# Layer 0's front with TensorE in a written order: pairs of tiles mixed on quarter blocks, and a tail written out by hand on all engines

## The chip, the cores and the metric

The kernel runs on one core of a Trainium2 chip. The core has a matrix engine (TensorE, PE), a vector engine (VectorE, DVE), a scalar engine (ScalarE, ACT), a general engine (GpSimd, POOL) and an engine that issues transfers (SyncE, SP); every engine works through its own queue of instructions in order and waits on semaphores for the others. Matmuls read from the on-chip memory SBUF and write to PSUM, which has eight banks of 512 f32 columns on 128 partitions.

The metric is the time of the whole program on the device, in microseconds. The kernel before took 2567.02 us in the median of three runs (2560.18 to 2570.76).

## The reference

The program computes four layers, each a conditional linear map ("cond") followed by a block ("ffn"), on 2048 tokens of 512 numbers, all in f32. The change lies in layer 0 and, by one constant, in the front of layer 1. Layer 0 is this:

```python
# cond: sequences of 64 tokens, each with its own 64x64 weights, over the tokens
w = weights[conditions]                       # 200 sets of weights, 32 sequences
x = einsum('bct,bcd->bdt', x, w)              # B, 64, 512
# attention, sequences of 64 here (causal), 16 heads of 32
n = rmsnorm(x, ln1)
kv, q = n @ kv_d_w, n @ q_d_w                 # latents of 128
k = concat(kv @ k_u_w, rope(n @ rope_k_w));  q = concat(q @ q_u_w, rope(q @ rope_q_w))
h = x + (softmax(mask(q k^T / sqrt(32))) @ (kv @ v_u_w)) @ o_w
# mixture of experts: one shared expert, two of seven routed ones per token
n = rmsnorm(h, ln2)
probs = sigmoid(n @ router_w + router_b);  scores, idx = top_k(probs, 2)
out = h + shared(n) + sum_k scores_k / sum(scores) * expert[idx_k](n)
# expert(x) = (silu(x @ wg) * (x @ wu) / 8) @ wd, inner size 256
```

Layer 1 begins with a cond of the same form (8 sets of weights), and a router with 32 experts, four per token.

## The kernel before, in words

The 2048 tokens are 16 tiles (NT) of 128 tokens, that is, two sequences a tile. Layer 0 has a *front* (class `Front`), which does all up to the routing of every tile, then an expert stage, which gathers the rows that belong to each expert (`xr`, L361, issued on POOL), multiplies them (gu L1191, y L1204) and writes them out.

The front is a software pipeline. A loop over 19 steps calls 13 methods in each step, each for the tile of its own lag (table `turns`): lag 0 is the newest tile, lag 3 the oldest. In the order of the table: `mix` (0), `values` (2), `qk_turn` (1), `norm_turn` (0), `out_turn` (2), `gate_up` (3), `scores` (1), `latents` (0), `out` (2), `down` (3), `qkv` (0), `probs_turn` (1), `out_norm` (2). Apart from that the tile framework's planner sets the order of each engine's queue; it moves instructions by what it takes their costs to be.

What the methods are, with the line that the profile shows:

- `mix` (L605): both 64x64 weights of a tile are gathered into `wsel` (L361, POOL), and POOL lays them out as a 128x128 matrix with two blocks on its diagonal (`wbd`, L418, two operations). One matmul of 128x128 weights with 512 columns, in two f32 passes, mixes the tile. ScalarE copies it to `h` (L607); `rms_scaled` squares it on ScalarE (L395), VectorE scales the sum (ms, L397), POOL takes the power (rstd, L385) and VectorE makes `xn` (L400).
- `turn` (L587) transposes a tile by four matmuls into one bank; VectorE (L589, L593) or ScalarE (L591) copies it to SBUF. `norm_turn` turns xn, `qk_turn` q and k (qT, kT), `probs_turn` the probabilities (sT), `out_turn` the attention's result, `out_norm` the normed `hn`.
- `latents` is lp (L631, 16 passes), `qkv` is qp (L644 to L650) and vp (L669: four matmuls with 128x64 weights, two column halves), `scores` is sp (L698) and the softmax on VectorE (L703, m L708, the subtraction L709, den L712) and ScalarE (exp L710). `values` is ap (L731), 64x64 weights in the four quarters of the array; VectorE divides (att, L738, two halves). `out` is op (L756), eight passes of 512 columns, then the sum, the norm and the store of `hn` as a row of `rows`.
- `gate_up` is the router's matmul rp (L776, tile name tok), sigmoid (L781), the two largest (`choose`, L969 and L970), and the shared expert's gate and up (gu, L506). `down` is the shared expert's y (L796), and after every second tile the `put`.
- `put` (L976 to L1004, L941 to L964) counts where each token of two tiles goes: VectorE makes `hot` (L979), `sel` (L984), `pre` (L986); two matmuls (L989, L990) count; VectorE goes on with the count to the one-hot tables `a` and `b` (L950), ScalarE scales `a` (L961), and four f16 matmuls (`total`, L963) add to the lists of tokens, which `end` casts to `stok`. The gathers of the expert stage read `stok`.

The tag "one" in PSUM has three banks for mix, tp, lp, vp, op, gu and y together; "big" has two pairs of banks for qp, sp and ap; one bank holds the router's and the put's small results.

Tiles in LATER (6 to 13) leave out the shared expert in the front: it is done afterwards, for the first two (GAP) in the gap before layer 1, for the others in *pieces* between the steps of layer 1's front (class `Mixed`, L243 in the profile, `fill`): six pieces a tile, four of gu and two of y. Tiles in SPLIT (0 to 10) have their router's matmul in layer 1 done as four column parts of 32 (`parts`), copied by ScalarE and added by a second matmul; the others have one direct matmul.

`g.held` is a set of engines whose instructions stay in the order in which the program gives them; `g.nc` leaves the order to the planner.

Of the kernel before, what the change touches and what calls it, by code (L numbers as in the profile page):

```python
# [21 lines left out]
P = 128  # L22
# [21 lines left out]
LATER = range(6, NT - 2)  # L44
LEAD = 6
GROUPS = {3: 4, 7: 4, 11: 4, 13: 2, 15: 2}
SPLIT = range(11)
# [98 lines left out]
def _layout(i):  # L146
# [7 lines left out]
    a["cond0"] = i["itok_B_1_198"].reshape(NT, 2).T  # L154
# [269 lines left out]
def layer0(g, w3, pool3):  # L424
    tc, nc, a = g.tc, g.nc, g.a
    with ExitStack() as ctx:
# [6 lines left out]
        with ExitStack() as c1:  # L433
# [3 lines left out]
            x = [g.load_x(sb, a["x"], i, 5) for i in range(3)]  # L437
# [8 lines left out]
            f = Front(g, sb, ps, w, br, ln2, at0, m, x, xs, shared)  # L446

            turns = (
                ("mix", 0), ("values", 2), ("qk_turn", 1), ("norm_turn", 0), ("out_turn", 2), ("gate_up", 3),
                ("scores", 1), ("latents", 0), ("out", 2), ("down", 3), ("qkv", 0), ("probs_turn", 1),  # L450
                ("out_norm", 2),
            )
            for step in range(NT + 3):
                if step >= 4:
                    clear()
                if step in (15, 17):
                    m.weights((step - 15) // 2)
                for stage, lag in turns:
                    if 0 <= step - lag < NT:
                        getattr(f, stage)(step - lag)  # L460
            m.end(sb)
        m.ready(ctx)
# [103 lines left out]
class Front:  # L566
# [3 lines left out]
    def __init__(self, g, sb, ps, w, br, ln2, at, m, x, xs, shared):  # L570
        self.shared = shared
        self.g, self.sb, self.ps, self.w, self.br, self.ln2 = g, sb, ps, w, br, ln2
        self.at, self.m, self.x, self.xs = at, m, x, xs
        self.held = {}
# [7 lines left out]
    def turn(self, src, dst, act, scale=None):  # L582
# [3 lines left out]
        for c in range(4):  # L586
            nc.tensor.transpose(tp[:, c, :], src[:, c * P : (c + 1) * P], self.g.ident)  # L587
# [7 lines left out]
    def mix(self, i):  # L595
        g, nc, sb = self.g, self.g.nc, self.sb
        if i == 0:
            self.weights(0)
            self.lay()
        wbd = self.wbd  # L600
        if i >= len(self.x):
            self.x.append(g.load_x(sb, g.a["x"], i, 5))
        x = self.x[i]
        o = self.ps.tile([P, D], F32, name="mix", tag="one")
        nc.tensor.matmul(o, wbd, x, start=True, stop=True)  # L605
        h = sb.tile([P, D], F32, name="h", bufs=4)
        nc.scalar.copy(h, o)  # L607
        self.keep(i, x=x, h=h, xn=g.rms_scaled(sb, h, "xn", True))
        self.weights(i + 1)

    def weights(self, i):

        self.asked = self.g.cond_weights(self.sb, "wc0", self.at, i) if i < NT else None

    def lay(self):
        if self.asked:
            self.wbd = self.asked(self.sb.tile([P, P], F32, name="wbd"))
# [7 lines left out]
    def latents(self, i):  # L625
# [3 lines left out]
        for j in range(2):  # L629
            for c in range(4):  # L630
                nc.tensor.matmul(  # L631
                    lp[:, j, :], w["w_lat"][:, c, j * P : (j + 1) * P], xnT[:, c, :], start=c == 0, stop=c == 3
                )
# [3 lines left out]
        self.lay()  # L637

    def qkv(self, i):
        g, nc, sb, w = self.g, self.g.nc, self.sb, self.w  # L640
# [3 lines left out]
        nc.tensor.matmul(qp[:, 0, :], lat[:, 1, :], w["w_q"], start=True, stop=True)  # L644
        kv = qp[:, 1, :].rearrange("p (h z d) -> p z h d", h=16, z=2)
        nc.tensor.matmul(
            kv[:, 0], lat[:, 0, :], w["w_kn"].rearrange("p (h d) -> p h d", h=16), start=True, stop=True
        )
        for c in range(4):
            nc.tensor.matmul(  # L650
# [16 lines left out]
        for b in range(2):  # L667
            for odd in range(2):
                nc.tensor.matmul(  # L669
# [15 lines left out]
    def scores(self, i):  # L685
# [5 lines left out]
        for rr in range(2):  # L691
            sp = self.ps.tile([P, 2, D], F32, name="sp", tag="big", bufs=2)
            for r2 in range(2):
                q0 = 32 * (2 * rr + r2)
                for c in range(4):
                    for b in range(2):
                        cols = slice(64 * b, 64 * b + 64)
                        nc.tensor.matmul(  # L698
# [12 lines left out]
        den = sb.tile([P, 16], F32, name="den", bufs=3)  # L711
        nc.vector.tensor_reduce(den, s, AX.X, ALU.add)  # L712
        nc.vector.reciprocal(den, den)
        self.keep(i, s=s, den=den)
# [8 lines left out]
    def values(self, i):  # L723
# [3 lines left out]
        for j in range(8):  # L727
            for odd in range(2):
                rows = slice(64 * odd, 64 * odd + 64)
                for b in range(2):  # L730
                    nc.tensor.matmul(  # L731
# [18 lines left out]
    def out(self, i):  # L750

        g, nc, sb = self.g, self.g.nc, self.sb
        attT, h, x = self.take(i, "attT", "h", "x")
        op = self.ps.tile([P, D], F32, name="op", tag="one")
        for c in range(4):
            nc.tensor.matmul(op, attT[:, c, :], self.w["w_o"][:, c, :], start=c == 0, stop=c == 3)  # L756
        nc.vector.tensor_tensor(h, h, op, ALU.add)
        hn = g.rms_scaled(sb, h, "hn")
# [12 lines left out]
    def gate_up(self, i):  # L771
        g, nc, sb, w = self.g, self.g.nc, self.sb, self.w
        (hT,) = self.take(i, "hnT")
        rp = self.m.bank[:, 448 : 448 + E0]
        for c in range(4):
            nc.tensor.matmul(rp, hT[:, c, :], w["w_r0"][:, c, :], start=c == 0, stop=c == 3)  # L776
        lg = sb.tile([P, E0], F32, name="lg")
        nc.vector.tensor_tensor(lg, rp, self.br, ALU.add)
        probs = sb.tile([P, 8], F32, name="probs")
# [3 lines left out]
        if i == NT - 1:  # L783
            self.m.put(self.sb, i - 1, 2)
        if i not in LATER:
            self.shared.hT[i] = hT
            self.shared.up(sb, self.ps, i, "one")

    def down(self, i):
        nc = self.g.nc  # L790
        if i not in LATER:
            (x,) = self.take(i, "x")
            act = self.shared.acts.pop(i)
            y = self.ps.tile([P, D], F32, name="y", tag="one")
            for ic in range(2):
                nc.tensor.matmul(y, act[:, ic, :], self.w["w_shd"][:, ic, :], start=ic == 0, stop=ic == 1)  # L796
            nc.vector.tensor_tensor(x, x, y, ALU.add)
            nc.sync.dma_start(out=self.xs[i * P : (i + 1) * P, :], in_=x)
        if i % 2 and i < NT - 1:
            self.m.put(self.sb, i - 1, 2)  # L800
# [44 lines left out]
class Moe:  # L845
# [90 lines left out]
    def mark(self, sb, ps, tok, sl, slot, ov, i, n, tiles):  # L936
# [1830 lines left out]
```

## Time and profile before

| what | value |
|---|---|
| median of three runs | 2567.02 us (2560.18 to 2570.76) |
| profiled execution | 2568.85 us |
| its span, and what lies around it | 2567.1 us and 1.75 us |
| mean granted TensorE clock | 0.975 |
| TensorE busy | 2430.8 us (95% of the span) |
| VectorE, ScalarE, GpSimd busy | 1408.3, 715.5, 908.4 us |
| steady part of layer 0's front, 60 to 345 us | TensorE busy 274.69 of 285 us |
| end of the front and first experts, 345 to 396 us | TensorE busy 39.23 of 51 us, clock 0.74 |
| layer 1's front, 640 to 700 us | TensorE 50.14, VectorE 50.10 of 60 us |
| start of the values of tile 14 (ap, the first work of the last steps) | 331.94 us |
| first gather of rows for the experts | 376.21 us |

How to read it: PE is the matmul, PEld the load of its weights, which runs beside the matmuls. Every f32 matmul is two records, since it is two passes. A line of a timeline has the start in us, the busy time, engine, line, operation, result and inputs, the shapes, and in square brackets the idle time of the engine just before with what ended it. A line of the waits has in the end the sum in us, how often, and the longest. In the rows by stretches each engine has its busy us and, in parentheses, its number of instructions; behind them stand the granted clock (1 is full speed), the share of the DMA engines and GB/s.

### The profile page before, as it was taken

How to read it: one execution, taken by the hardware profiler on the slowest of the kernel's cores; microseconds unless marked ns; L12 is line 12 of the kernel's file. 1: busy time of each engine (PE TensorE's matmuls, PEld its weight loads, DVE VectorE, ACT ScalarE, POOL GpSimd, SP SyncE). 2: the span in 40 equal slices, each digit the busy share in tenths (PEclk: the TensorE clock that was granted, in tenths of full speed). 3: DMA queues.
4: the chain of work that ended last, by engine and by line, in shares of the span. 5: the costliest groups of instructions: out<-in, count | busy, mean ns of one | idle time of the engine just before them, and what ended most of it. 6: DMA issues, size and time to landing. Idle time of an engine off the chain costs nothing.

```text
span 2567.1 us, 42539 instructions
## 1 busy us (share of the span) xinstructions
PE 2430.8 (95%) x16597; PEld 1624.3 (63%) x16597; DVE 1408.3 (55%) x3470; ACT 715.5 (28%) x1480; POOL 908.4 (35%) x961
## 2 busy tenths in 40 slices
PE   6999989998889999969999999999999999979998
PEld 4776766665566666746666666666666665435665
DVE  4667656832855554436554444455444432557887
ACT  2444420111311111101322222222222221236664
POOL 2223225613243444533333333333333212573440
PEclk9999989999989999989999999999999999989999
DMA  2334325435556877844222222222222213523551
GB/s 102 105 126 169 112 71 196 157 133 175 202 170 230 344 275 255 293 161 163 66 77 76 76 76 73 73 73 73 76 77 76 82 55 135 166 69 110 146 143 54
DMA packets 132570, 339.40 MB, mean 132 GB/s; under 512 B 23993, under 2 KB 25049, under 8 KB 125056
## 3 DMA queue, kind: packets, MB, share of 16 engines
q1 hardware_dynamic: 90720, 188.84, 21.5%
q0 software_dynamic: 41056, 141.89, 17.5%
q10 hardware_dynamic: 576, 5.77, 0.6%
q8 instruction: 136, 2.23, 0.4%
q14 instruction: 82, 0.67, 0.1%
HBM read 245.23 MB, written 107.22 MB: 137 GB/s over the span
## 4 chain that ended last, share of the span: by engine, by line
PE 50%; DVE 2%; POOL 1%; issue 1%; DMA 1%; ACT 0%; SPq 0%; ACTq 0%; POOLq 0%; DVEq 0%
PE out L2138 9%; PE lp L1997 8%; PE zp L2074 8%; PE pp L2453 3%; PE hp L2106 3%; PE gp L2129 3%; PE y L2702 2%; PE yp L1940 2%; PE sp L2632 2%; PE pT L2654 2%; PE op L2680 2%; PE ep L2083 1%; PE kp L2605 1%; PE ap L1928 1%; PE out L2144 1%
## 5 line engine op out<-in xcount | busy, mean ns | idle before, releaser
L1191 PE MATMUL gu<-xT,wt 128*128 128x320 f32 (+5 forms) x1536 | 399.2, 407 | 5.2 <-issue 3.5
L1191 PEld LDWEIGHTS gu<-xT,wt 128*128 128x128 f32 x1536 | 284.7, 194 | 119.3 <-issue 52.6
L1997 PEld LDWEIGHTS lp<-xnT,sb_mu 128*128 128x128 f32 x2048 | 235.0, 193 | 10.7 <-issue 6.7
L1997 PE MATMUL lp<-xnT,sb_mu 128*128 128x128 f32 x2048 | 238.0, 276 | 3.5 <-DVE xnT L333 2.9
L2138 PE MATMUL out<-sb_w,gT 128*128 128x512 f32 x512 | 234.9, 602 | 0.0
L2074 PE MATMUL zp<-sb_w,xnT 128*128 128x512 f32 x512 | 226.5, 592 | 0.0
L1204 PE MATMUL y<-wt,hT 128*128 128x512 f32 (+2 forms) x544 | 199.9, 595 | 1.3 <-DVE yo L1212 0.7
L361 POOL DMA_INDIRECT kvst<-kv,gidx x96 | 94.9, 988 | 272.9 <-DMA oldkv<-kvst 196.6
L2074 PEld LDWEIGHTS zp<-sb_w,xnT 128*128 128x128 f32 x512 | 93.7, 190 | 104.8 <-issue 102.2
L2138 PEld LDWEIGHTS out<-sb_w,gT 128*128 128x128 f32 x512 | 92.2, 190 | 96.1 <-issue 92.8
L361 POOL DMA_INDIRECT kvt<-newkv,oidx x96 | 100.3, 1045 | 111.0 <-PE pT L2654 37.7
L361 POOL DMA_INDIRECT yk<-ys,slot x96 | 97.6, 1017 | 118.1 <-DVE pre L1300 74.4
L2133 DVE COPY gT<-gp 128x512 f32<-128x512 f32 x64 | 44.2, 691 | 168.2 <-PE gp L2129 168.2
L1204 PEld LDWEIGHTS y<-wt,hT 128*128 128x128 f32 (+2 forms) x544 | 72.8, 166 | 63.6 <-issue 50.3
L361 POOL DMA_INDIRECT xr<-rows,stok x101 | 98.0, 970 | 41.1 <-issue 18.5
L841 POOL TENSOR_TENSOR ga<-ga,sg 128x288 f32<-128x288 f32 (+5 forms) x66 | 50.8, 770 | 170.5 <-ACT sg L837 168.5
L2111 ACT ACTIVATE h<-hp 128x512 f32<-128x512 f32 x128 | 73.1, 597 | 120.3 <-PE hp L2106 105.7
L2085 ACT COPY ew<-ep 128x512 f32<-128x512 f32 x64 | 37.2, 583 | 200.5 <-PE ep L2083 193.9
L2035 POOL TENSOR_TENSOR eT<-eT,inv 128x512 f32<-128x512 f32 x64 | 67.0, 1050 | 72.6 <-DVE inv L2034 67.0
L2002 DVE TENSOR_TENSOR lT<-lp,cmu 128x512 f32<-128x512 f32 x64 | 44.1, 690 | 79.7 <-PE lp L1997 79.7
L2643 ACT ACTIVATE s<-s,m 128x336 f32<-128x336 f32 x128 | 72.7, 569 | 46.0 <-DVE m L2639 39.7
L2026 ACT ACTIVATE eT<-eT 128x512 f32<-128x512 f32 x64 | 40.3, 630 | 156.6 <-DVE eT L2023 152.7
(458 smaller groups left out, 4614.4 us busy)
## 6 DMA issues: line engine op xcount, KB each, us to landing
ys<-yo SPq DMA_DIRECT2D x106, 256.0 KB
oldkv<-kvst SPq DMA_DIRECT2D x96, 224.0 KB
kvt<-oldkv SPq DMA_DIRECT2D x96, 224.0 KB
ys<-zero SPq DMA_DIRECT2D x10, 2048.0 KB
xt<-x SPq DMA_DIRECT2D x62, 256.0 KB
x<-xt SPq DMA_DIRECT2D x48, 256.0 KB
wt<-w_e SPq DMA_DIRECT2D x7, 1536.0 KB
sb_w<-w SPq DMA_DIRECT2D x5, 1024.0 KB
```

Source lines behind the costliest of these rows:

```text
L361: ins = self.nc.gpsimd.indirect_dma_start(out=out, out_offset=None, in_=src, in_offset=bass.IndirectOffsetOnAxis(ap=idx, axis=0), **kw)
L1191: follow(nc.tensor.matmul(o, wj[:, c, ic * P : (ic + 1) * P], xTs[u][:, c, 0:n], start=c == 0, stop=c == 3))
L1204: follow(nc.tensor.matmul(y[row : row + n, :], hTs[e][:, ic, col : col + n], wd[:, ic, :], start=ic == 0, stop=ic == 1,))
L1997: g.first(e + c, nc.tensor.matmul(lp[:, e, :], w["mu"][:, c, (4 * q + e) * P : (4 * q + e + 1) * P], self.xnT[:, c, :], start=c == 0, stop ...
L2035: g.pin(nc.gpsimd.tensor_tensor(e3, e3, inv.unsqueeze(2).to_broadcast([P, 8, T]), ALU.mult))
L2074: g.first(c, nc.tensor.matmul(zp, self.xnT[:, c, :], w["w1"][:, c, cols], start=c == 0, stop=c == 3))
L2106: g.first(e + b, nc.tensor.matmul(hp[:, b, e, :], self.ews[q][r, e, :], self.z[q][r, e * P : (e + 1) * P], start=True, stop=True))
L2111: g.pin(nc.scalar.activation(self.hs[q][b], hp[:, b], AF.Gelu))
L2129: g.first(e + b + k, nc.tensor.matmul(gp[r, e, cols], self.hs[q][b][:, e, r], self.lT[q][:, e, cols], start=True, stop=True))
L2138: g.first(e, nc.tensor.matmul(self.out, self.gTs[q][:, e, :], w["w2"][:, 4 * q + e, :], start=False, stop=q + e == 6 and q == 3))
L2453: nc.tensor.matmul(pp, xT[i][:, c, :], (w["w_kv3"] if z else wq)[:, c, :], start=c == 0, stop=c == 3)
L2643: nc.scalar.activation(p, p, AF.Exp, bias=m, scale=-1.0, accum_out=tot)
```

## The change

TensorE's instructions in layer 0's front are given through `g.held.tensor`, so that their order is that of the program. The table `turns` is longer: `gate_up` is split into `route`, `chosen` and `gate_up`; `out` into `out`, `summed`, `scaled`, `normed`; den is `weigh`; `put` is a generator whose parts are called as `chosen` (up to pre), `count` (the two matmuls, then VectorE's and ScalarE's work) and `sum` (the total). `norm_turn` stands behind `out_turn` and `gate_up`, and `count` stands ahead of `out`.

`mix` runs in even steps for two tiles. It multiplies with the gathered 64x64 weights as they are, in the four quarters of the array: for the first tile rows 0 to 63 to partitions 0 to 63 and rows 64 to 127 to partitions 64 to 127; for the second crosswise, for which its x is loaded a second time with the halves swapped (`xw`, two transfers of 64 rows), and its two indices are swapped in `cond0`. `wbd` is gone.

The loop ends with step 15. The rest (tiles 13, 14, 15) is `tail`, one sequence in which all compute engines are held. LATER is 6 to 12 instead of 6 to 13, so tile 13's shared expert is done in the tail; SPLIT is 0 to 8 instead of 0 to 10. The second set of expert weights is asked for ahead of the tail instead of at step 17, and `stok` is cast (`listed`) ahead of the last two y matmuls.

```diff
-LATER = range(6, NT - 2)
+LATER = range(6, NT - 3)
-SPLIT = range(11)
+SPLIT = range(9)
...
-    a["cond0"] = i["itok_B_1_198"].reshape(NT, 2).T
+    c0 = i["itok_B_1_198"].reshape(NT // 2, 2, 2)
+    a["cond0"] = np.stack((c0[:, 0], c0[:, 1, ::-1]), 1).reshape(NT, 2).T
...
+            def swapped(i):
+                if i < NT:
+                    other[i] = sb.tile([P, D], F32, name="xw")
+                    for k in range(2):
+                        r = i * P + 64 * (1 - k)
+                        g.dma(other[i][64 * k : 64 * k + 64, :], a["x"][r : r + 64, :], later=False)
...
             turns = (
-                ("mix", 0), ("values", 2), ("qk_turn", 1), ("norm_turn", 0), ("out_turn", 2), ("gate_up", 3),
-                ("scores", 1), ("latents", 0), ("out", 2), ("down", 3), ("qkv", 0), ("probs_turn", 1),
-                ("out_norm", 2),
+                ("mix", 0), ("values", 2), ("sum", 3), ("qk_turn", 1), ("route", 3), ("chosen", 3), ("out_turn", 2),
+                ("gate_up", 3), ("norm_turn", 0), ("scores", 1), ("weigh", 1), ("latents", 0), ("count", 3), ("out", 2),
+                ("summed", 2), ("scaled", 2), ("normed", 2), ("down", 3), ("qkv", 0), ("probs_turn", 1), ("out_norm", 2),
             )
-            for step in range(NT + 3):
+            for step in range(NT):
...
-                if step in (15, 17):
-                    m.weights((step - 15) // 2)
+                if step == 15:
+                    m.weights(0)
...
+                load(step + 3)
+                if step % 2:
+                    swapped(step + 2)
+            m.weights(1)
+            plain, g.nc = g.nc, SimpleNamespace(**{**vars(g.held), "sync": g.nc.sync})
+            f.tail()
             m.end(sb)
+            g.nc = plain
...
     def mix(self, i):
+        if i % 2:
+            return
...
-        o = self.ps.tile([P, D], F32, name="mix", tag="one")
-        nc.tensor.matmul(o, wbd, x, start=True, stop=True)
-        h = sb.tile([P, D], F32, name="h", bufs=4)
-        nc.scalar.copy(h, o)
...
+        outs = [self.ps.tile([P, D], F32, name="mix", tag="one") for _ in range(2)]
+        for t, src in ((0, self.x[i]), (1, self.other.pop(i + 1))):
+            w = self.asked.pop(i + t)
+            for k in range(2):
+                r = slice(64 * k, 64 * k + 64)
+                o = 64 * (k ^ t)
+                self.pe.matmul(outs[t][o : o + 64, :], w[r, :], src[r, :], start=True, stop=True)
+        for t in range(2):
+            h = sb.tile([P, D], F32, name="h", bufs=4)
+            nc.scalar.copy(h, outs[t])
+            self.keep(i + t, h=h, xn=g.rms_scaled(sb, h, "xn", True))
+        self.weights(i + 2)
...
+    def count(self, i):
+        if i % 2:
+            next(self.put)
+            next(self.put)
+
+    def sum(self, i):
+        if self.put and i % 2 == 0:
+            next(self.put, None)
+            self.put = None
...
+    def tail(self):
+
+        a, b, c = NT - 3, NT - 2, NT - 1
+        self.values(b)
+        self.qk_turn(c)
+        self.out_turn(b)
+        self.route(a)
+        self.scores(c)
+        self.out(b)
+        self.up(a, (0, 1))
+        self.summed(b)
+        self.weigh(c)
+        self.up(a, (2,))
+        self.probs_turn(c)
+        self.up(a, (3,))
+        self.scaled(b)
+        self.normed(b)
+        self.values(c)
+        self.out_norm(b)
+        self.chosen(a)
+        self.act(a)
+        self.out_turn(c)
+        self.route(b)
+        self.out(c)
+        next(self.put)
+        self.down_rows(a)
+        self.chosen(b)
+        self.up(b, (0, 1, 2))
+        self.summed(c)
+        next(self.put)
+        self.scaled(c)
+        self.normed(c)
+        self.out_norm(c)
+        self.down_sum(a)
+        self.up(b, (3,))
+        self.route(c)
+        next(self.put, None)
+        self.chosen(c)
+        self.up(c, (0, 1))
+        next(self.put)
+        next(self.put)
+        self.up(c, (2, 3))
+        self.act(b)
+        next(self.put, None)
+        self.m.listed()
+        self.down_rows(b)
+        self.act(c)
+        self.down_rows(c)
+        self.down_sum(b)
+        self.down_sum(c)
```

## The prediction

> **What bounds the kernel now.** I read the page first, then the busy time by stretches, then the waits of TensorE in the pipelined part of the front, then timelines of single steps and of the tail.
>
> ```profile
> PE 2430.8 (95%) x16597; PEld 1624.3 (63%) x16597; DVE 1408.3 (55%) x3470; ACT 715.5 (28%) x1480; POOL 908.4 (35%) x961
> PEclk9999989999989999989999999999999999989999
> ```
>
> TensorE is busy for 95% of the whole, and the clock row dips where it is not: slice 6 (320 to 385 us) is the end of layer 0's front. By stretches (columns: TensorE, weight load, VectorE, ScalarE, GpSimd, granted clock, DMA):
>
> ```profile
> 60.00:345.00 285.00, 274.69 (x3194) 204.51 (x3194) 190.44 (x490) 130.19 (x222) 76.83 (x104) 0.99 0.34 117
> 345.00:396.00 51.00, 39.23 (x215) 33.17 (x215) 20.38 (x83) 5.63 (x15) 15.85 (x18) 0.74 0.39 132
> 640.00:700.00 60.00, 50.14 (x347) 35.49 (x347) 50.10 (x134) 19.01 (x39) 18.73 (x17) 1.00 0.64 217
> ```
>
> In the steady part of the front only 285 - 274.7 = 10.3 us are idle; in 51 us of tail and first expert work 11.8 us are idle and the clock is 0.74. Layer 1's front has VectorE as busy as TensorE. In the steady part TensorE waits for this:
>
> ```profile
> PE tp L587 <- DVE xn L400: 5.3, 10, 0.9
> PE tp L587 <- issue: 1.0, 2, 0.5
> PE tp L587 <- ACT kT L591: 0.5, 1, 0.5
> ```
>
> These are 13 waits of one place, the turn of the normed tile: 6.8 us. A step with a LATER tile and a put looks like this, VectorE first, then TensorE:
>
> ```profile
> 226.60 1.22 DVE L708 TENSOR_REDUCE m<-s 128x16 f32<-128x1024 f32 x1
> 227.74 0.18 DVE L979 TENSOR_TENSOR hot<-sb_cst,chosen 128x28 f32<-128x28 f32 x1
> 227.86 1.22 DVE L709 TENSOR_TENSOR s<-s,m 128x1024 f32<-128x1024 f32 x1
> 229.00 0.18 DVE L984 TENSOR_REDUCE sel<-hot 128x14 f32<-128x28 f32 x1
> 229.21 0.37 DVE L986 TENSOR_TENSOR pre<-pre,sel 128x7 f32<-128x7 f32 x2
> ```
>
> ```profile
> 226.28 1.49 PE L631 MATMUL lp<-xnT,sb_w_lat 128*128 128x128 f32 x11 [0.60 <-issue]
> 227.61 3.60 PE L756 MATMUL op<-sb_w_o,attT 128*128 128x512 f32 x8
> 231.05 0.29 PE L989 MATMUL tok<-pre,sb_cst 128*128 128x14 f32 x2
> ```
>
> `pre` is ready at 229.58 and its matmul runs at 231.05: the 3.44 us of op are its cover. The put's `pre` stands on VectorE behind two softmax passes of 1.22 us.
>
> **The change part by part.** A step is a tile's pass; LATER steps are those from step 9 on.
>
> *The turn of xn* moves behind the attention turn and gate_up. Its 6.8 us of waits go: -6.8.
>
> *Mix.* Seven pairs run in steady steps. A tile's mix is now two passes of 0.43 us; a pair would be 0.86 instead of 1.72 if all four quarters run at once, 1.72 if two do, 3.44 if none. Nearest is vp, two column halves:
>
> ```profile
> 215.56 1.08 PE L669 MATMUL vp<-sb_w_v,lat 128*64 128x256 f32 x8
> ```
>
> Eight passes of 0.215 us (1.72 in a row) took 1.08, so two at a time is shown, and I take four. But the second mix bank is freed by VectorE's sT, about 0.45 us after the first: 7 x (0.86 - 0.45) = -2.9. The Trainium skill, "TensorEngine Tiling (Array Packing)", section Gotcha 1, speaks against it: row tiles can't access one PSUM bank at the same time, and both row halves write each mix bank here; by that rule a pair is about 2.6 us, and the sum below would be some 12 us longer. No row before shows two row groups on one bank.
>
> *New waits in even steps.* The changed queues of VectorE have, after a pair: ms, xn, half of att, ms of the second tile, other half of att, second xn, qT. Laid out with the durations above from mix's end: h 0.59, square 0.82, h 0.59, square 0.82 on ScalarE give the second ms at 3.0; att ends at 3.6; TensorE has only ap 1.06, qk turn 0.93 and route 0.90 = 2.9 to do before it turns att. That is 0.9 us, 7 times: +6.3 (nothing if ScalarE takes the first tile early, 1.3 if late). qT, behind the second xn, is then late for the scores by 0.45 in the LATER steps (in earlier ones gate_up covers it): 3 x 0.45 = +1.4.
>
> *count before op.* In steps 10, 12 and 14 VectorE still has `pre` behind m and the subtraction, at scores' start + 6.2 us (rows above: 229.58 - 223.36; the other two puts of this kind are the same within 0.1). TensorE now reaches count at scores' start + 3.25 (scores 1.50, lp 1.75). So op, and everything behind it, waits 3.0 us: 3 x 3.0 = +9.0. In steps 4, 6 and 8 gate_up (3.5 us) stands between, and `pre` is in time. Lower bound 0, if VectorE gets to `pre` early; upper 3.44, the cover lost.
>
> *Put's total* moves behind ap and gets a second buffer. Steps with a put are now 0.6 to 1.0 us longer than those without (24.0, 23.7 against 23.0 between lp starts), LATER ones 1.8 to 2.4 (19.5, 20.1 against 17.74), of which matmuls are 0.56: 3 x 0.3 + 3 x 1.5 = -5.4.
>
> *POOL and SP.* 32 wbd operations of 0.44 go from POOL; nobody waits for them, the cover is POOL's idle time. Two wsel gathers of 1.27 stand together behind two rstd, used two steps later. SP gets 16 more issues of 128 KB (0.33 us each); in the built queue each stands some steps ahead of its mix, covered by whole steps of 17 us; without that a mix would wait behind a store of zeros (2048 KB at some 380 GB/s, 5.5 us). At the start tile 1's two loads precede the weights and wbd's 0.87 goes: 0, within 1 either way.
>
> Loop: -6.8 - 2.9 + 6.3 + 1.4 + 9.0 - 5.4 = +1.6.
>
> *The tail.* Before, from the start of ap(14) at 331.94 to the first gather of rows at 376.21: 44.3 us, with gaps like these
>
> ```profile
> 346.31 0.22 PE L963 MATMUL tok<-a,b 128*128 128x35 f16 x2 [2.37 <-ACT a L961]
> 363.94 0.63 PE L587 MATMUL tp<-sb_cst,hn 128*128 128x128 f32 x4 [1.53 <-DVE hn L400]
> 365.36 1.57 PE L776 MATMUL tok<-sb_w_r,hnT 128*128 128x7 f32 x8 [0.78 <-DVE hnT L589]
> 374.50 0.44 PE L963 MATMUL tok<-a,b 128*128 128x35 f16 x4 [0.71 <-ACT a L961]
> ```
>
> and passes at half rate (gu takes 5.52 us for 32 passes, 3.74 in 366 to 370 for 16). After, with full-rate durations: ap 2 x 1.06, qk turn 0.9, att turns 1.1, routes 2.7, scores 1.5, op 2 x 3.44, gu of three tiles 10.3 (tile 13's is new), tp s 0.9, tp hn 0.9, counts 0.8, y(13) 1.7 (new), totals 0.5 = 30.3 us. Waits in the written order: 1.5 for the second put's chain (count, 2.3 of VectorE, 0.5 of ScalarE) ahead of its total, 0.4 each for hn(14) and att(15), 0.7 of small ones: 33.3. Then tokens and stok behind tile 14's act on VectorE: gather at 34.8. y(14) and y(15) end at about 37.9, beside the gather's landing (3.5 us in the rows of before, 376.2 to 379.75). So -9.5. Bounds: -4 with half-rate windows as before, -13 if the waits vanish. The second weights move past SP's later stores, earlier; the experts' first turn waits for rows, not for them.
>
> *Layer 1's front.* Tile 13's six pieces (5.2 us of TensorE) leave it. Without pieces a step is 4.1 us (687.29 to 691.37 between mixes) against 4.67 with (664.67 to 669.34), as VectorE (50.1 of 60 us) and the chain of turns set it: two steps x 0.6, and VectorE's 0.85 for the tile: -2 (0 to -5.2). Direct logits of tiles 9 and 10 are 8 passes instead of 8 and 2 with a copy: nothing, as that copy's wait goes with them.
>
> Sum: +1.6 - 9.5 - 2 = -9.9 against the profiled execution, 2568.85 us (span 2567.1 and 1.75 around it), which is 1.8 above the median 2567.02. That gives 2559 us.
>
> **Rivals.** (a) *The queues give way and the loop gains.* If `pre` comes before the softmax passes in effect, or att is in time, the +9.0 and half of +7.7 go: 2559 - 13 = 2546. For it: the rows show both operands depend on nothing but short operations. Against: VectorE works in queue order. (b) *Quarters do not run at once.* Two at a time adds 0.86 x 7 = 6: 2565; one at a time 2.58 x 7 = 18: 2577. For: no row shows it; against: vp. (c) *Slower, by the clock.* The 3 us holes at count drop the granted clock. A hole of 2.4 us at 343.9 to 346.3 stood in a half-rate stretch of 10.3 us (345.2 to 355.5), which costs up to 5.1 us. Three such are +15, 2574. It decides from 9.9 us, two such stretches; holes of 1.9 and 2.15 us in layer 1 (656, 677) cost no clock, which speaks against. (d) *The tail's gain is lost later*: the expert stage, which has gaps for rows and half rate until 396 anyway, takes the 9.5 back: 2568, as if nothing were changed. Against: its first turn waits for the gather directly.
>
> **How the numbers follow.** Main case 0.45, own range 2552 to 2566; (a) 0.32; (b) 0.08; (c) 0.10; (d) 0.05. About 0.5%, 12.8 us, is what a measurement tells from no change, so faster is below 2554.2 and slower above 2579.9. Faster: 0.30 from (a) and 0.07 of the main case's lower edge; slower: 0.04 of (c) and 0.03 of (b). The range of 8 in 10 reaches to (a) and (c): 2542 to 2574. The likeliest is 2559.
>
> **What would show it.** Right: waits of the xn turn gone; three waits of about 3 us ahead of the pre matmul in LATER even steps; waits of about 0.9 ahead of the att turn in even steps; a pair of mixes under 1.5 us from first to last; gathers of rows about 35 us after ap(14). Wrong: `pre` ready before lp ends; mixes over 2 us; a clock under 0.95 in the steady part; new waits for rows or weights at the experts' start.

## The result and the profile after

The changed kernel takes 2568.03 us in the median of 20 runs (2562.26 to 2574.10), the kernel before 2565.65 in 20 runs (2558.46 to 2570.76). The ratio is 1.0013 with a 95% interval of 1.0004 to 1.0022: 3 us slower, a little more than nothing. Forecast was 2559, so neither the sign nor the size came. That the time lies in the stated range of 2542 to 2574 is owed to the range's width, not to the working.

The profiled execution took 2569.69 us, its span 2567.9, 0.8 more than before. *Half rate* means, here and below, a stretch in which the trace's granted clock is 0.5. The page of the changed kernel, TensorE's work and its clock:

```profile
PE 2436.4 (95%) x16610; PEld 1629.8 (63%) x16625; DVE 1416.9 (55%) x3471; ACT 710.2 (28%) x1475; POOL 891.9 (35%) x928
PEclk8999899999889999989999999999999999989999
```

Busy time by stretches of the changed kernel (columns as in the prediction, the last three granted clock, DMA share, GB/s):

```profile
0.00:60.00 60.00, 38.76 (x339) 28.53 (x340) 20.92 (x44) 13.78 (x26) 11.52 (x18) 0.83 0.73 263
60.00:345.00 285.00, 278.42 (x3205) 210.56 (x3204) 188.57 (x475) 125.80 (x217) 61.67 (x75) 0.97 0.27 97
345.00:396.00 51.00, 41.23 (x297) 30.94 (x296) 29.09 (x105) 8.37 (x21) 16.38 (x22) 0.92 0.31 102
640.00:700.00 60.00, 49.40 (x310) 33.73 (x308) 49.20 (x132) 19.04 (x37) 17.74 (x16) 0.93 0.65 223
```

The tail has most of the clock that the sum took for it: 0.92 instead of 0.74. But the first 60 us have a clock of 0.83 instead of 1.00, and the steady part 0.97 instead of 0.99. TensorE is *busier* there (278.4 of 285 us instead of 274.7) and gets no further: between the marks below it works at half rate for 17.1 us instead of 6.8. TensorE's waits in the steady part of the changed kernel:

```profile
PE tp L244 <- DVE att L768: 3.6, 6, 0.6
PE tok L244 <- DVE pre L1128: 1.2, 2, 0.7
PE sp L244 <- DVE qT L620: 1.0, 3, 0.3
PE sp L244 <- issue: 0.8, 2, 0.4
```

The waits for xn are gone, and the three new ones stand where the prediction put them, for att, pre and qT, each smaller than forecast. Where the time went shows by marks in the two traces (starts, in us):

| mark | before | after | difference | its stretch | forecast |
|---|---|---|---|---|---|
| latents of tile 3 | 70.3 | 76.8 | +6.5 | start: +6.5 | 0 |
| values of tile 14 | 331.9 | 338.8 | +6.9 | loop: +0.4 | +1.6 |
| first gather of rows | 376.2 | 377.5 | +1.3 | tail: -5.6 | -9.5 |
| first mix of layer 1 | 610.2 | 612.6 | +2.4 | experts: +1.1 | 0 |
| first fixed list of layer 1 | 715.2 | 716.4 | +1.2 | layer 1's front: -1.2 | -2 |
| end of the span | 2567.1 | 2567.9 | +0.8 | rest: -0.4 | 0 |

In the start, lp of the kernel before takes 2.05 us:

```profile
34.87 2.05 PE L631 MATMUL lp<-xnT,sb_w_lat 128*128 128x128 f32 x16
```

The start of the changed kernel:

```profile
36.47 3.36 PE L244 MATMUL lp<-xnT,sb_w_lat 128*128 128x128 f32 x16
...
45.54 0.65 PE L244 MATMUL mix<-xt,wsel 64*64 64x512 f32 x2
45.85 0.65 PE L244 MATMUL mix<-xw,wsel 64*64 64x512 f32 x2
46.02 0.60 PE L244 MATMUL mix<-xt,wsel 64*64 64x512 f32 x2
46.33 0.59 PE L244 MATMUL mix<-xw,wsel 64*64 64x512 f32 x2
46.45 1.38 PE L244 MATMUL ap<-v,sT 64*64 64x32 f32 x64
...
50.29 0.63 PE L244 MATMUL tp<-sb_cst,att 128*128 128x128 f32 x4 [1.44 <-DVE att L768]
...
54.34 3.78 PE L244 MATMUL lp<-xnT,sb_w_lat 128*128 128x128 f32 x16
57.92 4.49 PE L244 MATMUL op<-sb_w_o,attT 128*128 128x512 f32 x8
```

A pair's eight passes run from 45.54 to the start of ap at 46.45: 0.91 us for two tiles, all four quarters at once. lp takes 3.36 and 3.78 us instead of 2.05. The trace's granted clock is 0.5 from 32.4 to 39.2 and from 52.9 to 59.7 (and, ahead of these rows, from 18.7 to 25.5); before, it is 1 from 24.4, where its record begins, to 280.4. The same follows every put step of a LATER tile, at 230.4 (3.4 us), 267.9 (3.4) and 305.5 (10.2):

```profile
225.95 0.63 PE L244 MATMUL tp<-sb_cst,att 128*128 128x128 f32 x4 [0.60 <-DVE att L768]
226.41 0.60 PE L244 MATMUL tp<-sb_cst,xn 128*128 128x128 f32 x4
227.34 1.45 PE L244 MATMUL sp<-kT,qT 32*64 32x64 f32 x50 [0.33 <-DVE qT L620]
229.18 0.67 PE L244 MATMUL sp<-kT,qT 32*64 32x64 f32 x14 [0.40 <-issue]
229.78 3.28 PE L244 MATMUL lp<-xnT,sb_w_lat 128*128 128x128 f32 x16
233.78 0.39 PE L244 MATMUL tok<-pre,sb_cst 128*128 128x14 f32 x2 [0.72 <-DVE pre L1128]
```

Here lp at half rate hides most of the wait for pre, 0.72 us instead of the 1.95 that the run `old_constants` below shows at full rate: the hole is filled with slow work.

### The profile page after: what moved, and what is told of

The parts are those of the page before. It is cut to its first block, busy times and chain, and to the rows that moved or that the text cites. A ratio compares the mean times of both kernels' runs of the same rounds, so it can differ in the third digit from the quotient of the medians.

```text
span 2567.9 us, 42551 instructions
## 1 busy us (share of the span) xinstructions
PE 2436.4 (95%) x16610; PEld 1629.8 (63%) x16625; DVE 1416.9 (55%) x3471; ACT 710.2 (28%) x1475; POOL 891.9 (35%) x928
## 4 chain that ended last, share of the span: by engine, by line
PE 48%; DVE 3%; issue 1%; DMA 1%; POOL 1%; ACT 1%; SPq 0%; ACTq 0%; POOLq 0%; DVEq 0%
PE out L2281 9%; PE lp L2140 8%; PE zp L2217 8%; PE pp L2596 3%; PE hp L2249 3%; PE gp L2272 3%; PE yp L2083 2%; PE y L2845 2%; PE sp L2775 2%; PE pT L2797 2%; PE op L2823 1%; PE ep L2226 1%; PE kp L2748 1%; PE out L2287 1%; PE ap L2071 1%
## 5 line engine op out<-in xcount | busy, mean ns | idle before, releaser
L1347 PEld LDWEIGHTS y<-wt,hT 128*128 128x128 f32 (+2 forms) x544 | 72.8, 166 | 62.8 <-issue 50.7
```

Source lines behind the costliest of these rows:

```text
L1347: follow(nc.tensor.matmul(y[row : row + n, :], hTs[e][:, ic, col : col + n], wd[:, ic, :], start=ic == 0, stop=ic == 1,))
```

## The experiments

Two theories at first. **Q**: VectorE works in queue order, and what stands ahead of att, qT and pre opens holes on TensorE, which cost time and clock. **S**: the loop is TensorE's own work, and the loss is that pairs suit an empty pipeline badly. Ratios are to the kernel before on the same chip; the changed kernel's is 1.0013. Not all runs share a chip, and each trace is one execution, so marks of two traces differ by their half rate as well as by the edit.

### The orders of count and of VectorE

```diff
-("latents", 0), ("count", 3), ("out", 2),
+("latents", 0), ("out", 2), ("count", 3),
```

> The changed kernel with one edit: count stands behind out again. Theory Q (VectorE's queue order leaves TensorE holes, and the holes also drop its clock): the three half-rate stretches behind the put steps of LATER tiles (230.4 to 233.8, 267.9 to 271.3, 305.5 to 315.7 us, 17.1 us in all) and the waits for pre (1.2 us) go, the values of tile 14 start 5 to 9 us earlier than the 338.8 of the changed kernel, and the whole is 4 to 8 us faster than it. Theory S (only the start of the pipeline and the tail differ; the loop is bound by TensorE's own work): tile 14's values start within 2 us of 338.8 and the time is the same as that of the changed kernel.

Measured: 0.9993 (0.9977 to 1.0009). The waits for pre are gone, half rate in the loop is 6.8 us instead of 17.1, tile 14's values start at 332.5, 6.3 earlier, of which 1.8 are from the start. In the profiled execution layer 1's front took 112.8 us instead of 103.8 and gave it back; on the median 0.2% are left, with intervals that overlap. At the marks this is theory Q's outcome. How much is the order's own and how much the clock's is open: `old_constants` below has count ahead of out, no half rate, and a loop of 257.4 us, this run 6.8 us of half rate and 257.5.

```diff
 # mix: copies and squares only; then
+# values:   att (first half), mean of tile i, att (second half)
+# qk_turn:  qT
+# units:    xn of tile i, mean and xn of tile i + 1, then the gathers of wsel
+# att, means and xn on g.held.vector
```

> The changed kernel with VectorE's order written out around a mixed pair: both halves of att and qT ahead of the xn of the first tile and of the mean and xn of the second. Theory Q: the waits of TensorE's att turn (3.6 us between 60 and 345, 1.4 before 60) go to under 1 us, the scores' wait for qT too, so that tile 14's values start 4 to 8 us earlier than at 338.8, and the wait for pre grows back by what the scores come earlier (to 1 to 3 us a put step). Theory S: xn is late instead, the waits move to the turn of xn, tile 14's values start within 2 us of 338.8.

Measured: 0.9970 (0.9953 to 0.9986). No wait for att or qT of over 0.4 us is left; for pre 1.7 in two waits. Tile 14's values start at 326.0; from tile 3's latents to there it is 253.7 us instead of 262.0. xn is not late. This is the largest single effect, and theory S has nothing to explain it with. Of the 12.8 us at tile 14's values, 4.5 are from the start, and part of the loop's gain may be clock (half rate of 6.8 us instead of 17.1); `att_old_constants` below compares two loops without half rate.

> Both edits together: count behind out, and VectorE's order around a pair written out. Theory Q: no wait for att, qT or pre of over 0.3 us is left, no half-rate stretch between 60 and 340 us, tile 14's values start at 325 to 331 us, and the whole takes 8 to 13 us less than the changed kernel, 0.3 to 0.5 percent less than the kernel before. Theory S: same as the changed kernel within 3 us.

Both edits: 0.9964 (0.9946 to 0.9982). The loop takes 253.3 us, no less than with VectorE's order alone: with att early, pre is early enough to cost little. Half rate of 6.8 us remains in the loop, which Q did not expect, and the start fell on 76.9.

### The parts undone

```diff
-self.pe.matmul(outs[t][o : o + 64, :], w[r, :], src[r, :], start=True, stop=True)   # pairs
+self.pe.matmul(o, self.wbd, self.x[i], start=True, stop=True)                       # one tile a step
```

> The changed kernel with one tile mixed per step by the block-diagonal weights, as before; order of TensorE, tail and constants as changed. If the pairs cost the start (theory S): the latents of tile 3, at 76.8 us in the changed kernel and at 70.3 in the kernel before, come back to 69 to 72 us, and tile 14's values start 4 to 8 us earlier than at 338.8. If the start is lost to the held order itself: the latents of tile 3 stay at 75 to 78 us. In the loop a pair saved about 0.86 us of matmul, so each even and odd pair of steps is 0.3 to 0.9 us longer here unless theory Q holds, in which case the even steps are shorter by the lost waits for att (0.6 each).

Measured: 1.0087 (1.0059 to 1.0114). Tile 3's latents start at 72.8 us, just over S's 69 to 72, with 3.4 us of half rate between 25 and 60. That doesn't show that pairs cost the start: with pairs and the same 3.4 us, `no_tail` below is at 70.6. The loop takes 281.2 us, 30.7 of them at half rate. Its waits are others, for the put, as VectorE's queue comes out in another order:

```profile
PE tok L243 <- DVE tokens L1099: 6.8, 6, 1.4
PE tok L243 <- DVE pre L1121: 6.2, 3, 2.1
PE tp L243 <- DVE att L761: 2.6, 7, 0.4
```

So this run doesn't tell what pairs are worth by themselves.

```diff
-nc.tensor.matmul(...)            # all of Front, put and total, in the kernel before
+self.g.held.tensor.matmul(...)
```

> The kernel before with nothing changed but that TensorE's instructions in layer 0's front are held in the order of the program (the old table, single mixes, old constants, no written tail). If the held order as such opens holes: tile 14's values start later than the 331.9 us of before by 4 us or more, with new waits in every step. If it does nothing by itself: 330 to 334 us, latents of tile 3 at 70 to 72 us, the time within 3 us of before.

Measured: 1.0238 (1.0215 to 1.0261), with medians 55 us apart. The order of the program as it was is not one that TensorE can be held to:

```profile
PE tok L243 <- ACT a L961: 30.9, 7, 5.1
PE tp L243 <- DVE xn L400: 11.2, 13, 1.2
```

The put's total stands right behind its count there and waits up to 5.1 us for VectorE and ScalarE; the planner had moved it. In the changed kernel, with the generator, `sum` a step later and `norm_turn` moved, neither wait is left in the loop. So they are no extras; they weren't taken away one by one.

### Constants and tail

```diff
-LATER = range(6, NT - 3); SPLIT = range(9)
+LATER = range(6, NT - 2); SPLIT = range(11)     # and tile 13's up, act, down out of tail()
```

> The changed kernel with LATER 6 to 13 and SPLIT 0 to 10 again, so that tile 13's shared expert goes back to layer 1's front. If the tail is TensorE's own work, as the prediction took it: from tile 14's values to the first gather of rows 33 to 34.5 us instead of 38.7 in the changed kernel; layer 1's front (first mix of layer 1 to the first fixed list) 105 us, 1 more than its 103.9, so the whole is 3 to 5 us faster than the changed kernel. If the tail is bound by the chain of tile 15 (norm, router, put), the work of tile 13 lay in its waits: the tail stays at 37 to 39 us and the whole is within 2 us of the changed kernel.

Measured: 1.0002 (0.9984 to 1.0021). The tail takes 38.6 us, no less without tile 13's 5.2 us of matmul: TensorE's waits up to the second total are 6.3 us there instead of 2.9, 4.1 of them for hn instead of 1.9, and 7.2 us are at half rate instead of 3.8. Its loop, the same program as the changed kernel's, ran without any half rate in this execution and shows the put step as it is:

```profile
226.98 2.05 PE L244 MATMUL lp<-xnT,sb_w_lat 128*128 128x128 f32 x16
230.98 0.39 PE L244 MATMUL tok<-pre,sb_cst 128*128 128x14 f32 x2 [1.95 <-DVE pre L1122]
```

The wait for pre is 1.9 us, three times (5.8 in all), and the loop takes 257.4 us: 4.2 less than before (which has 6.8 us of half rate in it), 4.6 less than with 17.1 us at half rate.

> The changed kernel without the written-out tail: its loop runs on through steps 16 to 18 with the table's order on TensorE and the planner's on the other engines, tile 13's shared expert among it. From tile 14's values to the first gather: 46 to 50 us if the tail's order is what saved time there (before, without tile 13's 5.2 us, it was 44.3), so 8 to 11 us slower than the changed kernel as a whole. If holding TensorE's order was enough: 39 to 41 us and within 2 us of the changed kernel.

The loop runs on through steps 16 to 18 and `tail()` is gone. Measured: 1.0017 (1.0002 to 1.0032). From tile 14's values to the first gather it takes 51.7 us, 13 more than with the tail; but from there to layer 1's first mix 228.6 instead of 235.1. Half of the tail's gain at the gather is spent behind it: in the changed kernel y of tiles 14 and 15 (5.4 us) runs behind the gather, and a wait of 4.0 us for xT at 393 stands where `no_tail` has none; `no_tail` waits 4.0 us for its first rows instead. On the median the written tail is not told from none.

> The kernel with VectorE's order around a pair written out, and LATER 6 to 13, SPLIT 0 to 10 as before. Theory Q with the clock: the front keeps the gain seen with that order (tile 14's values at 326 to 330 us), layer 1's front keeps its pieces and so its clock (105 to 106 us, against 107.3 with the order and the new constants), and the whole is 13 to 18 us under the kernel before, 0.5 to 0.7 percent. If the pieces do nothing for the clock: layer 1's front 107 or more, and the whole within 2 us of the run with the order alone (2558).

Measured: 0.9963 (0.9946 to 0.9980), as with the new constants (0.9970), and less than the 0.5 to 0.7 percent expected. The loop takes 249.7 us, the least of all, without half rate, on the chip of `old_constants`, whose 257.4 us are without half rate too: 7.7 us by VectorE's order alone, with no clock in it. The pieces changed nothing that can be told. In all five runs with the old constants a stretch of 6.8 us at half rate lies some 14 us behind tile 14's values (it begins at 334 to 347 us); in the runs with the written tail and tile 13 in it none begins there, though most have half rate elsewhere in the tail. That tile 13's work kept the clock there fits this and wasn't tested by itself.

### The clock

A third theory, C: half rate follows holes on TensorE, and which holes it follows is chance. The changed kernel was profiled again, and the kernel before, to see what is chance.

> The kernel before, profiled once more, to see whether its start and its half-rate stretches are the same from execution to execution. If the clock's windows fall by chance (theory C): the latents of tile 3 at 70 to 73 us, but the stretches elsewhere than at 280.4, 345.2, 365.7, 379.4 and 393.0. If they are set by the program: the same stretches within 3.4 us.

> The changed kernel, profiled once more. Theory C (the pairs leave holes in the start, and whether a hole costs the clock is chance): the latents of tile 3 anywhere from 70 to 77 us, with 3.4 to 20 us of half rate between 25 and 60. If the 6.5 us are the program's own waits: 76 to 77.5 us again.

Before: tile 3's latents at 69.5 us, the stretches at 281.8, 343.2, 363.7, 377.3 and 391.0, each within 2.1 us of the first profile's; the first is 3.4 us long instead of 6.8. Changed: 76.6 us, 13.6 us at half rate between 25 and 60, the loop's three stretches at 230.0, 267.5 and 305.1. So within a program it repeats, and pure chance, as I had put it, is wrong for these two. But four other runs have the same first steps as the changed kernel, instruction for instruction on TensorE, and all but count_after_op the same loop:

| run | half rate, 25 to 60 us | latents of tile 3 | half rate in the loop | loop |
|---|---|---|---|---|
| after | 14.2 us | 76.8 | 17.1 us | 262.0 us |
| after_again | 13.6 | 76.6 | 17.1 | 261.9 |
| count_after_op | 10.2 | 75.0 | (other loop) | |
| old_constants | 10.2 | 75.0 | 0 | 257.4 |
| layer1_fill (below) | 10.2 | 74.9 | 23.9 | 265.8 |
| no_tail | 3.4 | 70.6 | 13.7 | 260.2 |

The same start takes 70.6 to 76.8 us, and the time goes with the half rate, which comes in stretches of some 3.4 us or a multiple. Half rate can cost at most half its length (the loop below: 8.5 us of TensorE's own time for 17.1), so 5.4 of the 6.2 us between no_tail and after; 0.6 more is that the first lp starts earlier in no_tail (19.8 instead of 20.4). The loop's time goes with its half rate too. The holes are the program's; how many stretches follow them differs, on one chip too (old_constants and no_tail), and why isn't shown.

> The changed kernel with dummy 128x128 matmuls of the identity, whose result nobody reads, in TensorE's holes: 6, 7 and 6 in the first steps (ahead of the first turn of xn, the first turn of q and k and the first attention turn), 3 ahead of the attention turn of every later even step, 4 ahead of count from tile 5 on; 0.22 us each at full rate, 19 us of added work in the start and 0.66 to 1.5 us an even step. If the half-rate stretches are what the holes cost (theory C): no or one stretch between 25 and 60 us, latents of tile 3 at 70 to 73 us, none or one of 3.4 us behind the put steps, tile 14's values at 329 to 335 us, faster than the changed kernel by 2 to 6 us although work is added. If the holes' own length is what counts: tile 3's latents at 76 to 79 and tile 14's values later than 338.8.

```diff
+def fill(self, n):
+    for _ in range(n):
+        self.pe.matmul(self.m.bank[:, 64:192], self.g.ident, self.g.ident, start=True, stop=True)
```

The dummies add work and take none away (in the start 19 of 0.22 us, which is 4.2 us and not the 19 us of the text above). Measured: 1.0073 (1.0050 to 1.0097). In the start they do what the clock theory says: no half rate from 25 to 136 us, tile 3's latents at 68.3, with lp at its full rate:

```profile
32.29 2.05 PE L244 MATMUL lp<-xnT,sb_w_lat 128*128 128x128 f32 x16
...
48.46 2.05 PE L244 MATMUL lp<-xnT,sb_w_lat 128*128 128x128 f32 x16
```

In the loop the experiment failed by the way it was made: the dummies write to the bank that holds the router's result and wait until VectorE has read it:

```profile
PE tok L244 <- DVE lg L848: 12.7, 6, 2.4
```

Tile 14's values start at 344.5 us, with 20.5 us of half rate in the loop. So this run says nothing on the holes there. The next four were made for what it left open.

> The changed kernel with the dummy matmuls of the identity in the start alone: 6 ahead of the first turn of xn, 7 ahead of the first turn of q and k, 6 ahead of the first attention turn. If the start's loss is the clock's: no half-rate stretch between 25 and 60 us, latents of tile 3 at 68 to 69 us instead of 76.7, tile 14's values at 329 to 332, and the whole 0.2 to 0.35 percent faster than the changed kernel, that is 0.9980 to 0.9995 of the kernel before. If something later takes it back: the latents of tile 3 early, the whole within 0.1 percent of the changed kernel (1.0005 to 1.002).

Measured: 1.0000 (0.9985 to 1.0015). Tile 3's latents at 70.7 us, one stretch of 3.4 us at half rate at 50.0. The rows from 25 to 60 us, first of the changed kernel, then of this one:

```profile
25.00:60.00 35.00, 30.06 (x311) 23.52 (x311) 18.02 (x34) 9.72 (x18) 5.80 (x6) 0.80 0.63 232
```

```profile
25.00:60.00 35.00, 32.90 (x356) 24.88 (x355) 19.96 (x39) 11.22 (x21) 7.59 (x8) 0.95 0.63 234
```

6.1 us are won at that mark in the profile. In the ratio it is 0.13% or 3 us, less than expected, and the intervals overlap; layer1_fill below, on the same chip and without these dummies, has 0.9999. So the gain at the mark is shown, one for the whole program is not. (The profiled execution, 2553.46 us, is the shortest of its 12, whose median is 2564.87.)

> Count behind out, VectorE's order around a pair written out, and LATER 6 to 13, SPLIT 0 to 10 as before: the candidate to beat both kernels. By the runs so far: 0.36 to 0.55 percent under the kernel before; the wait for pre, 3.7 us in the run with VectorE's order and the old constants, under 1 us. If the gain of the orders is lost to the clock further on, 0.3 to 0.4 percent as each of the others.

Count behind out, VectorE's order and the old constants: 0.9955 (0.9941 to 0.9970).

> The best version so far (count behind out, VectorE's order around a pair written out, LATER 6 to 13 and SPLIT 0 to 10 as before; 0.9955 of the kernel before) with the dummies in the start. If the causes add: latents of tile 3 at 68 to 69 us instead of 71.2, first gather at 357 to 360, ratio 0.994 to 0.995. If not: 0.9955 or more.

The same with the dummies in the start: 0.9938 (0.9922 to 0.9953), the lowest ratio: 2549.76 us in the median beside 2563.33 for the kernel before. Tile 3's latents start at 69.8 us instead of 71.2, the first gather at 360.7, both just outside of what was expected. The interval overlaps that of the run without dummies, so that the causes add is not shown.

> The changed kernel with two dummy matmuls wherever layer 1's front has no piece left to put between its steps (about 25 times, 0.43 us each). If layer 1's front is slow there by the clock: half-rate time between 600 and 740 us under 20 instead of 44 to 61, layer 1's front (first mix to first fixed list) 97 to 101 us instead of 103.8 to 109.4, and the whole 0.1 to 0.3 percent faster than the changed kernel. If VectorE and the transfers set it: 104 to 110 us whatever the clock does.

```diff
 def fill(n=1):
+    if not pieces:
+        for q in range(2):
+            g.held.tensor.matmul(spare[0][:, q, :], g.ident, g.ident, start=True, stop=True)
```

Measured: 0.9999 (0.9984 to 1.0014). Half rate between 600 and 740 us fell to 20.4 us, as meant, but layer 1's front still took 102.6. Over all profiles but those of one chip it takes 99.7 to 112.8 us with 20 to 65 us at half rate, and 91.0 to 95.8 on the chip that ran old_constants, no_tail, held_before and att_old_constants. On this run's chip start_fill_after has more half rate, 44.4 us, and a shorter front, 99.7 us. So half rate alone doesn't set it; the dummies' own time is in the 102.6.

> The best version with both sets of dummies, start and layer 1. If both are the clock's: ratio 0.990 to 0.993, the fastest of all. If layer 1's front does not care for the clock: as start_fill_best within 0.001.

Measured: 0.9947 (0.9930 to 0.9965), no better than start_fill_best. Layer 1's front does not pay for dummies.

## Why the prediction was wrong

In the spans -9.9 us was forecast and +0.8 measured. The 10.7 us between them are 6.5 of the start, 3.9 of the tail, 1.1 of the experts and 0.8 of layer 1's front, less 1.2 of the loop and 0.4 of the rest.

**The start, the first step that failed.** "0, within 1 either way" counted loads and wbd. It measured +6.5 us. What I left out: in an empty pipeline the even steps' holes have nothing beside them (2.4 us for qk, 1.4 before; 1.4 for att), a mix that used to stand ahead of the first qk turn is gone, and half rate comes with such holes. With one stretch of 3.4 us of it the same start is at 70.6 us, 0.3 and 1.1 later than in the two profiles of the kernel before, and the stretch alone can cost 1.7, so the holes' own length cost next to nothing; with three or four it is at 74.9 to 76.8. That the holes bring the half rate is shown by the dummies in their place (68.3 us with no stretch, 70.7 with one), and that half rate is the time by lp's 3.36 and 3.78 us.

**The loop.** Forecast +1.6, measured +0.4: that these are close is luck. The loop between the marks, with TensorE's own time counted from each start to the next and its waits of over 0.15 us taken out:

| loop | half rate | TensorE's own time | its waits | all |
|---|---|---|---|---|
| before | 6.8 us | 254.0 us | 7.7 us | 261.6 us |
| changed | 17.1 | 255.5 | 6.5 | 262.0 |
| changed, no half rate (old_constants) | 0 | 247.0 | 10.4 | 257.4 |

- xn: the waits are gone, as forecast (-6.8; between the marks 6.2).
- Mix: four quarters at once, right, 0.91 us a pair. A tile alone takes 1.03 us before, from its start to the start of ap, not the 0.86 of the sum; and ap behind a pair takes 1.42 us instead of 1.07. A pair saves 0.80 us, where 0.41 was forecast: -4.7 for the loop's six pairs instead of -2.9 for seven. The rows are of the kernel before, then of old_constants; the times are from start to start:

```profile
237.48 1.10 PE L605 MATMUL mix<-xt,wbd 128*128 128x512 f32 x2
238.51 1.14 PE L731 MATMUL ap<-v,sT 64*64 64x32 f32 x64
239.58 0.66 PE L587 MATMUL tp<-sb_cst,qk 128*128 128x128 f32 x4
```

```profile
219.29 0.65 PE L244 MATMUL mix<-xt,wsel 64*64 64x512 f32 x2
...
220.20 1.49 PE L244 MATMUL ap<-v,sT 64*64 64x32 f32 x64
221.62 1.09 PE L244 MATMUL tp<-sb_cst,qk 128*128 128x128 f32 x8
```

- The rule that I weighed against four quarters at once (the Trainium skill, "TensorEngine Tiling (Array Packing)", Gotcha 1, by which row tiles can't access one PSUM bank at a time) does not show here: both row halves of a tile wrote one bank, and the pair took a third of the 2.6 us that I had worked out by it.
- att: 0.6 instead of 0.9 us, six times, 3.6 instead of 6.3. qT: 1.0 instead of 1.4. Place and mechanism right; VectorE's order alone, written out, gave 0.4%.
- count: 1.9 instead of 3.0 us a step, at full rate. I took pre's time from before, where it lay at scores' start + 6.2; in the changed queue it is at + 5.5 (230.98 - 225.49 in old_constants), and TensorE comes to count at + 3.5 instead of 3.25. In the profiled execution only 1.2 us in all are seen, as lp at half rate covers the rest.
- Put's total: -5.4 was forecast, and nothing of that size is there. TensorE waited for a total in neither loop, and the totals' matmuls take 0.6 us before and 0.7 after, in all six puts. What made those steps long before were single waits ahead of lp (0.6 us) and sp (0.8), half rate, and the put's matmuls, which stay.
- The clock: I had it as rival (c), at a tenth, and from the wrong rows. In the changed kernel's two profiles holes of 0.3 to 0.7 us beside the small matmuls of sp were followed by half rate three times of three; in old_constants, the same program, none of three were, holes of 1.95 us behind lp included, nor were layer 1's holes of 2 us, from which I argued. Half rate makes TensorE's own time 8.5 us longer, half of the 17.1, and the waits 3.9 shorter: it cost 4.6 us (262.0 against 257.4).

Without half rate the loop is 4.2 us faster than before. About 2.3 of these are the half rate in before's own loop (lp, op and sp are 2.3 us shorter); the other 2 are the change's.

**The tail.** -9.5 was forecast, -5.6 came. With a full clock it is 37.0 us (att_first, both_orders) against 34.8 worked out: the waits were right in sum (2.9 against 3.0), the matmuls took 32.2 instead of 30.3 (gu of three tiles alone 11.35 instead of 10.3), and act, lists and cast 1.9 instead of 1.5. Half rate added 1.7, all of it in op. Rival (d), that the experts take the gain back, came true by little more than 1 us: from the first gather to layer 1's first mix it takes 235.1 us instead of 233.9.

**Layer 1.** -2 forecast, -1.2 in the profiled pair; as this front differs by 6.7 us between two profiles of the kernel before and by 5.6 between two of the changed kernel, neither is shown.

What stays open: why some holes are followed by half rate and others, longer ones too, are not (sp's blocks of 32 by 64 stand in the loop's three, but no run took them away), and what sets layer 1's front.

## What to carry to other kernels

An order that is pinned on one engine must be followed through the queues of the others: here VectorE's order around a pair, written out, turned a loss of 0.1% into a gain of 0.3%, and pinning TensorE in the old table's order, put included, cost 2.4%. Price a hole not by its length alone but by what it does to the clock, look at the start of a pipeline by itself, and before taking such a loss for waits, compare the duration of the same instruction in both traces (lp, 2.05 or 3.36 us). A few dummy matmuls are a cheap test of that, if they share no bank with anything live; as a remedy for the whole program they are not clear of the noise here.

## What was not expected

- The same first steps took 70.6 to 76.8 us by how many 3.4 us stretches of half rate fell on them.
- Four 64x64 matmuls into two banks, both row halves on one bank, started within 0.3 us and took 0.91 us together.
- More work made a stretch faster: 13 dummies and a third set of 6 brought tile 3 from 76.8 to 68.3 us, and tile 13's 5.2 us in the tail cost it nothing (38.7 us with them, 38.6 without).
